# Where the side work of a mixture-of-experts stage is put between its pairs: fixed shares of a chunk instead of one interleaved list

## The chip, the cores and the metric

The kernel runs on one core of a Trainium2 chip. The time is the device time of one execution, in microseconds (us). The core has five engines with a queue of instructions each: TensorE (PE) multiplies matrices, VectorE (DVE) and ScalarE (ACT) work on elements, GpSimd (POOL) does some element work and issues some DMAs, and SyncE (SP) issues most DMAs. Each engine takes its own instructions in the order in which the program gives them, and waits for the others through semaphores.

## The reference

The input is an image batch of 2 x 256 channels x 64 x 64, read as two sequences of 4096 tokens. Three things are added to it in turn:

```
x = x + L0(gn(x))                  # a selective scan (Mamba), 256 channels
t = tokens(x)
t = t + attn(ln(t))                # a forward and a backward selective scan, 512 channels
t = t + ffn(ln(t))                 # the mixture of experts, the last stage below

def ffn(x):                        # x: 2 batches, 4096 tokens, 256 channels
    feat = mean(x, axis=0)         # over the two batches
    w = softmax(feat @ Wr + br)    # one weight per token and expert, 8 experts
    h = relu(bn(einsum('bfd,edh->bfeh', x, W1) + b1))
    h = relu(bn(einsum('bfeh,ehk->bfek', h, W2) + b2))
    y = einsum('bfeh,ehd->bfed', h, Wo) + bo
    return einsum('bfed,fe->bfd', y, w)
```

Every expert is computed for every token, and the router's weight w of a token is shared by the two batches, since it comes from their mean.

## The kernel before

Channels lie on partitions, 128 at a time (KC = 2 halves), and tokens are cut into 8 chunks of 512. The first and far longer part of the kernel runs the scans of all six jobs slot by slot. Into free slots it already places expert work for chunks whose tokens are finished, and stores each expert's unweighted result u in DRAM. In this kernel that covers all eight experts of batch 0 in every chunk, and of batch 1 in chunks 7 and 6.

The last stage, which the change touches, therefore has two kinds of chunk. `whole` holds chunks 7 and 6, of which everything is stored. `rest` holds chunks 5, 4, 3, 2, 1, 0, of which batch 1 is still to be computed. The stage walks over `pairs` (b, i, e), batch, chunk and expert: eight pairs, all of batch 1, for each chunk of `rest`, 48 in all. One turn of this loop does the following, in this order on every engine:

- `layer` twice (L1203): two halves with two matmuls each into a PSUM tile hp (L1208), and ACT's relu into h (L1212).
- `weigh` (L1218) of the pair before: DVE multiplies its h by the router's weights wb of its expert (L1219).
- `last_layer` (L1221) of the pair three turns back: eight matmul rows into y (L1227). After a chunk's eighth pair DVE adds y to x (L1232) and SP stores x to the output (L1182).
- Some items of the chunk's side work, a list of functions `side[i]`.

The side work consists of these items. `routes(j)` prepares the router of a chunk that comes later, in five steps:

- `load_n` (L1083): POOL issues the load of the normalized tokens n of both batches (L1093). A chunk that is already loaded is passed over.
- `layer_norm` (L1095): does nothing for a chunk whose normalized tokens were stored earlier, which is all but batch 1 of chunk 0.
- `both` (L1113): POOL adds the two batches into nm (L1115). There is one buffer of nm.
- `logits` (L1117): PE multiplies nm by Wr into lt (L1122); DVE, ACT (the exp, L1137) and DVE make the softmax w (L1127 to L1141).
- `spread` (L1143): PE transposes w (L1147), ACT copies it to wts (L1149), POOL writes that to DRAM (L1151) and loads it back to all partitions as wb (L1153, 2 MB). There are two buffers of wb.

`sums(j)` adds the stored results of a chunk to its tokens: `load_x` (SP loads x of both batches, L1163), `bias` (PE multiplies wts by bo, L1170; ACT copies, L1171; POOL adds it to x, L1173), then `add_early` for each stored expert (SP loads u, L1177; DVE multiplies it by wb, L1178, and adds it to x, L1179), and `store` (L1182) for a batch of which all experts were stored. A chunk of `rest` has 11 such items with eight adds, a chunk of `whole` 20 with sixteen. u has three buffers, x and n six each.

Before the change the list of chunk number `at` of `rest` is built at once (L1241 to L1254): first the sums of the whole chunk whose router was made during the chunk before, then the sums of the chunk itself mixed with the steps of `routes` of the next whole chunk and of the next chunk of `rest`, one step after every `every` sums. The loop takes an equal part of what is left after each pair (L1290); for the first chunk it begins after the third pair. So chunk 5 has the routes of 7 and 4, chunk 4 the sums of 7 and 4 and the routes of 6 and 3, chunk 3 the sums of 6 and 3 and the routes of 2; chunks 2 and 1 have their own sums and the routes of 1 and 0, and chunk 0 its own sums.

Of the kernel before, what the change touches and what calls it, by code (L numbers as in the profile page):

```python
# [131 lines left out]
def hybrid_kernel(ctx: ExitStack, tc: tile.TileContext, a: dict, out: bass.AP):  # L132
# [53 lines left out]
    with ExitStack() as st:  # L186
# [826 lines left out]
        done = []  # L1013
        for g in range(nq):
            i, jp, n = quads[g]
# [49 lines left out]
    with ExitStack() as st:  # L1065
# [11 lines left out]
        rest, whole = [], []  # L1077
# [5 lines left out]
        def load_n(i):  # L1083

            if (0, i) in n:
                return
            for b in range(NB):
                n[b, i] = mk.tile([P, KC, T], F32, tag="n", name=f"n_{i}{b}", bufs=6)
                if (b, i) in featured:
                    src = nf_dram[b][:, i, :, :]  # L1090
                else:
                    src = t_dram[b][:, :, i * T : (i + 1) * T]
                nc.gpsimd.dma_start(n[b, i], src)  # L1093

        def layer_norm(i):  # L1095
            for b in range(NB):
                if (b, i) in featured:
                    continue
                v = n[b, i]
                mean = psp.tile([P, T], F32, tag="ps", name=f"mean_m{i}{b}")  # L1100
                for k in range(KC):
                    nc.tensor.matmul(mean, mean_w, v[:, k, :], start=(k == 0), stop=(k == KC - 1))
                nc.vector.tensor_tensor(v, v, over_channels(mean), ALU.subtract)
                sq = mk.tile([P, KC, T], F32, tag="u", name=f"sq_{i}{b}", bufs=3)
                nc.scalar.activation(sq, v, AF.Square)
                var = psp.tile([P, T], F32, tag="ps", name=f"var_m{i}{b}")
                for k in range(KC):
                    nc.tensor.matmul(var, mean_w, sq[:, k, :], start=(k == 0), stop=(k == KC - 1))
                r = mk.tile([P, T], F32, tag="r", name=f"r_{i}{b}", bufs=1)
                rsqrt(r, var, eps5)  # L1110
                nc.vector.tensor_tensor(v, v, over_channels(r), ALU.mult)

        def both(i):  # L1113
            n["sum", i] = mk.tile([P, KC, T], F32, tag="nm", name=f"nm_{i}", bufs=1)
            nc.gpsimd.tensor_tensor(n["sum", i], n[0, i], n[1, i], ALU.add)  # L1115

        def logits(i):  # L1117

            lt = psp.tile([P, q, E], F32, tag="ps", name=f"lt_{i}")
            for t in range(q):  # L1120
                for k in range(KC):
                    nc.tensor.matmul(  # L1122
                        lt[:, t, :], n["sum", i][:, k, t * P : (t + 1) * P], wr[:, k, :],
                        start=(k == 0), stop=(k == KC - 1),
                    )
            w = n["w", i] = mk.tile([P, q, E], F32, tag="w", name=f"w_{i}")
            nc.vector.tensor_tensor(  # L1127
                w, lt, br.rearrange("p (o e) -> p o e", o=1).to_broadcast([P, q, E]), ALU.add
            )
            mx = mk.tile([P, q], F32, tag="mx", name=f"mx_{i}")  # L1130
            nc.vector.tensor_reduce(mx, w, AX.X, ALU.max)

            def over_experts(v):
                return v.rearrange("p (q o) -> p q o", o=1).to_broadcast([P, q, E])

            nc.vector.tensor_tensor(w, w, over_experts(mx), ALU.subtract)
            nc.scalar.activation(w, w, AF.Exp)  # L1137
            sm = mk.tile([P, q], F32, tag="sm", name=f"sm_{i}")
            nc.vector.tensor_reduce(sm, w, AX.X, ALU.add)
            nc.vector.reciprocal(sm, sm)  # L1140
            nc.vector.tensor_tensor(w, w, over_experts(sm), ALU.mult)  # L1141

        def spread(i):  # L1143

            pt = psp.tile([P, T], F32, tag="ps", name=f"wt_{i}")
            for t in range(q):
                nc.tensor.transpose(pt[:E, t * P : (t + 1) * P], n["w", i][:, t, :], ident)  # L1147
            wts[i] = mk.tile([E, T], F32, tag="wt", name=f"wts_{i}", bufs=3)
            nc.scalar.copy(wts[i], pt[:E, :])  # L1149
            w_dram = drp.tile([E, T], F32, name=f"w_dram{i}")  # L1150
            nc.gpsimd.dma_start(w_dram, wts[i])  # L1151
            wb[i] = mk.tile([P, E, T], F32, tag="wb", name=f"wb_{i}")
            nc.gpsimd.dma_start(  # L1153
                wb[i], w_dram.rearrange("e (o t) -> o e t", o=1).to_broadcast([P, E, T])
            )

        def routes(i):
            return [lambda: load_n(i), lambda: layer_norm(i), lambda: both(i), lambda: logits(i), lambda: spread(i)]

        def load_x(i):  # L1160
            for b in range(NB):
                x[b, i] = mk.tile([P, KC, T], F32, tag="x", name=f"x_{i}{b}", bufs=6)
                nc.sync.dma_start(x[b, i], t_dram[b][:, :, i * T : (i + 1) * T])  # L1163

        def bias(i):

            bi = mk.tile([P, KC, T], F32, tag="bi", name=f"bi_{i}", bufs=1)
            for m in range(KC):
                ps = psp.tile([P, T], F32, tag="ps", name=f"bi_{i}_{m}")
                nc.tensor.matmul(ps, bo[:, m * P : (m + 1) * P], wts[i], start=True, stop=True)  # L1170
                nc.scalar.copy(bi[:, m, :], ps)  # L1171
            for b in range(NB):
                nc.gpsimd.tensor_tensor(x[b, i], x[b, i], bi, ALU.add)  # L1173

        def add_early(b, i, e):
            u = mk.tile([P, KC, T], F32, tag="u", name=f"u_{b}{i}_{e}", bufs=3)
            nc.sync.dma_start(u, u_dram[b, i, e])  # L1177
            nc.vector.tensor_tensor(u, u, over_channels(wb[i][:, e, :]), ALU.mult)  # L1178
            nc.vector.tensor_tensor(x[b, i], x[b, i], u, ALU.add)  # L1179

        def store(b, i):
            nc.sync.dma_start(  # L1182
                out[b].rearrange("(k p) l -> p k l", p=P)[:, :, i * T : (i + 1) * T], x[b, i]
            )

        def sums(i):

            work = [lambda: load_x(i), lambda: bias(i)]
            for b in range(NB):
                work += [lambda b=b, e=e: add_early(b, i, e) for e in range(first[b, i])]  # L1190
                if first[b, i] == E:
                    work.append(lambda b=b: store(b, i))
            return work
# [5 lines left out]
        def load_w(name, e):  # L1199
            we[name, e] = mw.tile([P, KC, C], F32, name=f"{name}_{e}")  # L1200
            nc.sync.dma_start(we[name, e], a[name][e].rearrange("(k p) n -> p k n", p=P))
# [16 lines left out]
        def weigh(b, i, e, h):  # L1218
            nc.vector.tensor_tensor(h, h, over_channels(wb[i][:, e, :]), ALU.mult)  # L1219
# [18 lines left out]
            (b, i, e) for i in rest  # L1238
            for e in (order if i == rest[0] else range(E)) for b in range(NB) if e >= first[b, i]
        ]  # L1240
        side = {i: [] for i in rest}  # L1241
        for at, i in enumerate(rest):
            after = rest[at + 1 : at + 2]
            now, work = sums(i), side[i]
            if at:
                for j in whole[at - 1 : at]:
                    work += sums(j)
            ahead = []
            for j in whole[at : at + 1] + after:
                ahead += routes(j)  # L1250
            every = max(1, len(now) // max(1, len(ahead)))
            while now or ahead:
                work += ahead[:1] + now[:every]
                ahead, now = ahead[1:], now[every:]  # L1254

        load_n(rest[0])
        for name, e in [("W1", order[0]), ("W2", order[0]), ("W1", order[1]), ("W2", order[1])]:
# [12 lines left out]
        done = {i: 0 for i in rest}  # L1270
        count = {i: sum(p[1] == i for p in pairs) for i in rest}
        for at, (b, i, e) in enumerate(pairs):
            for name, k in weights[: 6 if at else 4]:
                load_w(name, k)
            weights = weights[6 if at else 4 :]
            h = layer(n[b, i], 0, e, f"{i}_{e}_{b}")
            h = layer(h, 1, e, f"{i}_{e}_{b}")
            if at == 0:
                logits(i)
            elif at == 1:  # L1280
                spread(i)

            for p in {0: [], 1: [], 2: waiting[:1], 3: waiting[1:]}.get(at, waiting[-1:]):
                weigh(*p)
            waiting.append((b, i, e, h))
            if len(waiting) > 3:
                last_layer(*waiting.pop(0))
            done[i] += 1
            work = side[i] if at > 1 else []
            upto = -(-len(work) // (count[i] - done[i] + 1))  # L1290
            for fn in work[:upto]:
                fn()
            side[i] = side[i][upto:]
        weigh(*waiting[-1])
        for p in waiting:
            last_layer(*p)
# [104 lines left out]
```

## Time and profile before

| what | value |
|---|---|
| median of 3 runs | 5132.12 us (5131.54 to 5132.48) |
| the profiled execution | 5134.52 us |
| its span, first to last instruction | 5132.7 us |
| mean granted TensorE clock | 0.917 of full speed |
| busy: PE, DVE, ACT, POOL | 4283.0, 4581.7, 3681.3, 4410.3 us |
| last stage, 4537 to 5133 us: PE busy | 559.85 of 596 us |
| of these, chunk 5, 4537 to 4629 us: PE, DVE, ACT, POOL busy | 85.25, 34.44, 27.75, 16.88 us |
| chunk 4, 4629 to 4742 us | 97.25, 70.39, 28.74, 19.17 us |
| chunk 3, 4742 to 4844 us | 96.83, 73.71, 27.79, 14.72 us |
| chunks 2, 1 and 0, 4844 to 5133 us | 280.53, 101.74, 85.12, 24.90 us |

The profile is of one execution. A row of it names a line of the kernel, an engine, an operation and its tiles (output, arrow, inputs), with a time on that engine; an entry in square brackets tells how long the engine sat idle before the row and which instruction of which engine ended that wait. "SPq" is the time in which SP issues a DMA, not the time of its transfer. The times of the whole chunks in the table are windows of the timeline, cut at the first hp of a chunk.

### The profile page before, as it was taken

The numbers are of one execution on the slowest core, as the hardware profiler recorded it, in microseconds if no ns is written. First come the engines' busy times: TensorE is split into PE (matmuls) and PEld (weight loads), VectorE is DVE, ScalarE is ACT, GpSimd is POOL, SyncE is SP. The second block draws the span as 40 slices with busy tenths as digits, with TensorE's granted clock in tenths as the row PEclk, the third lists the DMA queues.
The fourth block names the chain that finished last, engine by engine and source line by source line (L and its number), as shares of the span: only waits on it lengthen the run. The fifth ranks groups of instructions, "written<-read, shape, count | busy, mean of one in ns | idle before, by whom it ended". The sixth has DMA issues, their size and how long they took to land.

```text
span 5132.7 us, 47350 instructions
## 1 busy us (share of the span) xinstructions
PE 4283.0 (83%) x14920; PEld 1485.7 (29%) x14920; DVE 4581.7 (89%) x3088; ACT 3681.3 (72%) x7474; POOL 4410.3 (86%) x1442
## 2 busy tenths in 40 slices
PE   5677767776668988888988888899999999888999
PEld 1222222221122323333322233233333333333444
DVE  6998999999999999999989999999999999936543
ACT  5777677777767888888888788888778878832232
POOL 5998999999999999999989999999999999911100
PEclk8888888887888999999999999999999999999999
DMA  5454433344444454546654555455554444455532
GB/s 178 149 176 158 164 136 128 132 146 144 151 139 156 170 195 163 184 165 209 207 185 170 174 181 179 159 167 177 195 187 166 167 165 161 168 180 182 191 108 77
DMA packets 321355, 845.49 MB, mean 165 GB/s; under 512 B 35720, under 2 KB 107152, under 8 KB 279120
## 3 DMA queue, kind: packets, MB, share of 16 engines
q1 hardware_dynamic: 316816, 815.07, 46.2%
q0 software_dynamic: 4288, 27.40, 1.4%
q8 instruction: 118, 1.93, 0.2%
q14 instruction: 133, 1.09, 0.1%
HBM read 655.05 MB, written 187.30 MB: 164 GB/s over the span
## 4 chain that ended last, share of the span: by engine, by line
DVE 20%; PE 15%; ACT 10%; issue 4%; POOL 3%; DMA 2%; SPq 0%; DVEq 0%; POOLq 0%; ACTq 0%
DVE da L690 9%; PE hp L1208 5%; DVE bq L699 5%; ACT da L664 4%; PE y L1227 2%; PE e L912 2%; DVE bq L690 2%; POOL bq L654 2%; PE conv L452 1%; POOL bq L715 1%; PE y L723 1%; ACT bq L675 1%; DVE x L1179 1%; DVE u L1178 1%; ACT eh L923 1%
## 5 line engine op out<-in xcount | busy, mean ns | idle before, releaser
L654 POOL TENSOR_TENSOR bq<-rxdt,bc 128x2048 f32<-128x2048 f32 x640 | 2893.2, 4543 | 28.7 <-issue 12.3
L664 ACT ACTIVATE da<-rdt,w_a 128x512 f32<-128x512 f32 x2560 | 1756.8, 686 | 105.4 <-DVE bq L690 59.8
L690 DVE TENSOR_TENSOR_SCAN da<-da,h_state,bq 128x1024 f32<-128x1024 f32 x664 | 1559.1, 2348 | 50.5 <-ACT da L664 34.4
L715 POOL TENSOR_TENSOR bq<-bq,bc 128x2048 f32<-128x2048 f32 (+1 forms) x280 | 1179.9, 4214 | 22.5
L690 DVE TENSOR_TENSOR_SCAN bq<-da,h_state,bq 128x1024 f32<-128x1024 f32 x456 | 1059.3, 2338 | 28.5 <-ACT da L664 28.4
L723 PE MATMUL y<-bq,stack 128*32 128x512 f32 x5120 | 759.4, 687 | 317.4 <-POOL bq L715 297.3
L699 DVE TENSOR_TENSOR bq<-da,bc 128x1024 f32<-128x1024 f32 x760 | 926.5, 1219 | 16.0
L912 PE MATMUL e<-eh,ew 128*128 128x512 f32 x1280 | 626.1, 620 | 66.0 <-DVE sp L513 15.0
L709 ACT COPY h_state<-da 128x2 f32<-128x2 f32 x759 | 119.1, 157 | 641.3 <-DVE bq L699 639.4
L675 ACT ACTIVATE bq<-h_state,bq,a 128x1 f32<-128x1 f32 x1120 | 430.5, 384 | 0.6
L723 PEld LDWEIGHTS y<-bq,stack 128*32 128x32 f32 x5120 | 143.6, 119 | 876.7 <-POOL bq L715 404.9
L1212 ACT ACTIVATE h<-hp,of,sc 128x512 f32<-128x512 f32 x192 | 149.1, 777 | 298.9 <-PE hp L1208 281.7
L912 PEld LDWEIGHTS e<-eh,ew 128*128 128x128 f32 x1280 | 230.3, 193 | 452.0 <-issue 219.4
L414 PE MATMUL xs<-nx,w_in 128*128 128x512 f32 x640 | 318.7, 628 | 40.9 <-DVE xc L466 20.8
L452 PE MATMUL conv<-xs,w_conv 64*64 64x512 f32 x2560 | 332.6, 613 | 21.9 <-ACT xs L436 18.9
L414 PE MATMUL z<-nx,w_in 128*128 128x512 f32 x640 | 323.8, 639 | 18.7 <-DVE sp L513 10.6
L912 PE MATMUL e<-en,ew 128*128 128x512 f32 x640 | 308.3, 613 | 23.9 <-DVE fcen L809 7.8
L761 PE MATMUL o<-sz,w_out 128*128 128x512 f32 x640 | 301.7, 612 | 0.0
L923 ACT ACTIVATE eh<-e,of,sc 128x512 f32<-128x512 f32 x320 | 242.1, 768 | 36.7 <-PE e L912 36.2
L517 POOL TENSOR_TENSOR xdt<-sp,xc 128x512 f32<-128x512 f32 x160 | 203.2, 1273 | 49.9 <-DVE sp L513 49.8
L730 PE MATMUL y<-xc,w_d 128*128 128x512 f32 x320 | 193.1, 688 | 54.2 <-DVE sz L742 53.9
L690 DVE TENSOR_TENSOR_SCAN da<-da,bq 128x1024 f32<-128x1024 f32 x96 | 219.4, 2286 | 6.5 <-ACT da L664 3.6
(139 smaller groups left out, 4940.5 us busy)
## 6 DMA issues: line engine op xcount, KB each, us to landing
rxdt<-xdtd SPq DMA_DIRECT2D x160, 1024.0 KB, 6.8
rdt<-dtd SPq DMA_DIRECT2D x160, 1024.0 KB, 6.5
bc<-bcd SPq DMA_DIRECT2D x384, 256.0 KB, 3.2
dtd<-sp SPq DMA_DIRECT2D x160, 256.0 KB, 3.5
xdtd<-xdt SPq DMA_DIRECT2D x160, 256.0 KB, 4.0
ew<-in_W SPq DMA_DIRECT2D x160, 256.0 KB, 4.3
u<-u SPq DMA_DIRECT2D x80, 512.0 KB, 4.4
u<-eu SPq DMA_DIRECT2D x76, 512.0 KB, 4.0
```

Source lines behind the costliest of these rows:

```text
L414: nc.tensor.matmul(ps, job.w["in", half][:, k, j * P : (j + 1) * P], rhs, start=(k == 0), stop=(k == KC - 1),)
L452: nc.tensor.matmul(v[r][64 * col : 64 * col + 64, :], job.w["conv"][rows, 2 * jp + j, k, :], ck["xs", jp][rows, j, k : k + T] if k < 4 els ...
L654: nc.gpsimd.tensor_tensor(bq[g], ck["rxdt", j], over_groups(ck["bc", 0, sg]), ALU.mult)
L664: nc.scalar.activation(da[g, h][:, k, :], cks[i]["rdt", j][:, q, :], AF.Exp, scale=steps[i][0].w["a"][:, j, q * SG + sg : q * SG + sg + 1],)
L675: nc.scalar.activation(bq[g][:, q, 0:1], job.h[:, j, sg, q : q + 1], AF.Identity, scale=cks[i]["a0", j][:, h, sg : sg + 1], bias=bq[g][:, ...
L690: nc.vector.tensor_tensor_scan(b if on_pool(g, h) else d, d, b, job.h[:, j, sg, 2 * h : 2 * h + 1] if c else 0.0, ALU.mult, ALU.add,)
L699: nc.vector.tensor_tensor(bq[g][:, two, :], d, cks[i]["bc", 1, sg].rearrange("p (o t) -> p o t", o=1).to_broadcast([P, 2, T]), ALU.mult,)
L715: nc.gpsimd.tensor_tensor(b, b, cks[i]["bc", 1, sg].rearrange("p (o t) -> p o t", o=1).to_broadcast([P, groups, T]), ALU.mult,)
L723: nc.tensor.matmul(y[i, j][q * CG : (q + 1) * CG, :], stack, bq[g][:, q, :], start=False, stop=(sg == SG - 1),)
L761: nc.tensor.matmul(v[m], job.w["out"][:, j, m * P : (m + 1) * P], ck["sz", j], start=False, stop=(j == job.nj - 1),)
L912: nc.tensor.matmul(ps, ew[l][:, k, m * P : (m + 1) * P], key[x][:, k, :], start=(k == 0), stop=(k == KC - 1),)
L923: nc.scalar.activation(key[dst][:, m, :], key["ps", l, m], AF.Relu, bias=of[:, l, e, m : m + 1], scale=sc[:, l, e, m : m + 1],)
```

## The change

The list of a chunk is now made of items with a share between 0 and 1, sorted by it. The five steps of `routes` get the shares 0, 0.2, 0.3, 0.55 and 0.8; where a whole chunk and a chunk of `rest` are both prepared, the second one's are 0.1 later. The sums, those of the whole chunk first as before, are spread evenly from 0.1 on. After each pair the loop runs every item whose share is below the part of the chunk's pairs that is done, and after the last pair all that is left. As before, the first chunk begins after its third pair. Nothing else is changed, and the same instructions are issued.

```diff
-        side = {i: [] for i in rest}
+        side = {}
         for at, i in enumerate(rest):
-            after = rest[at + 1 : at + 2]
-            now, work = sums(i), side[i]
+            side[i] = []
+            for k, j in enumerate(whole[at : at + 1] + rest[at + 1 : at + 2]):
+                for part, fn in zip((0, 0.2, 0.3, 0.55, 0.8), routes(j)):
+                    side[i].append((part + 0.1 * k, fn))
+            now = sums(i)
             if at:
-                for j in whole[at - 1 : at]:
-                    work += sums(j)
-            ahead = []
-            for j in whole[at : at + 1] + after:
-                ahead += routes(j)
-            every = max(1, len(now) // max(1, len(ahead)))
-            while now or ahead:
-                work += ahead[:1] + now[:every]
-                ahead, now = ahead[1:], now[every:]
+                now = [fn for j in whole[at - 1 : at] for fn in sums(j)] + now
+            side[i] += [(0.1 + 0.9 * k / len(now), fn) for k, fn in enumerate(now)]
+            side[i].sort(key=lambda work: work[0])
...
             done[i] += 1
-            work = side[i] if at > 1 else []
-            upto = -(-len(work) // (count[i] - done[i] + 1))
-            for fn in work[:upto]:
-                fn()
-            side[i] = side[i][upto:]
+            while at > 1 and side[i] and (done[i] == count[i] or side[i][0][0] < done[i] / count[i]):
+                side[i].pop(0)[1]()
```

## The prediction

> **What bounds the kernel now.** The page first: TensorE and VectorE share the load until the last stage, where the second half of the PE row is full and the DVE row falls off. I then asked for the chain of waits, restricted to the last stage (from 4537 us), for the waits of PE there, and for the timeline around each wait. In the chain, PE (L1208, L1227) carries the stage almost alone: a pair of batch and expert costs 10.57 us on PE (4652.20 to 4662.77), 48 pairs. What PE loses is in these waits (engine, line, what it waited for: us in total, times, longest):
>
> ```profile
> PE lt L1122 <- POOL nm L1115: 16.3, 2, 12.4
> PE hp L1208 <- DMA W<-in_W: 13.7, 1, 13.7
> PE wt L1147 <- DVE w L1141: 3.3, 2, 1.7
> PE var_m L1108 <- ACT sq L1105: 2.4, 1, 2.4
> PE hp L1208 <- ACT h L1212: 1.2, 1, 1.2
> ```
>
> The weight wait opens the stage and var_m belongs to the layer norm of the last chunk; neither is touched. The others lie in the second and third chunk (numbers 4 and 3). Timeline around the first (start, duration, what; in brackets idle before and its releaser):
>
> ```profile
> 4695.99 1.39 SPq L1163 DMA_DIRECT2D x<-t_dram  x2
> ...
> 4701.19 4.63 POOL L1173 TENSOR_TENSOR x<-x,bi 128x1024 f32<-128x1024 f32 x2 [53.21 <-DMA x<-t_dram]
> 4703.63 3.27 DVE L1178 TENSOR_TENSOR u<-u,wb 128x1024 f32<-128x1024 f32 x1 [6.97 <-DMA u<-u]
> 4705.79 3.31 POOL L1115 TENSOR_TENSOR nm<-n,n 128x1024 f32<-128x1024 f32 x1
> ...
> 4709.15 3.58 PE L1122 MATMUL lt<-wr,nm 128*128 128x8 f32 x16 [12.37 <-POOL nm L1115]
> ...
> 4712.77 0.19 DVE L1127 TENSOR_TENSOR w<-lt,br 128x32 f32<-128x32 f32 x1 [1.45 <-PE lt L1122]
> ```
>
> PE needs nm; nm stands on POOL behind the bias add of chunk 4, which waited for x; x was asked for late because SP stood behind sums that DVE had not done. Note that DVE itself reached the softmax of this lt only at 4711.3, where its last multiply before it (L1219, from 4710.10) ends. The second place shows what then happens:
>
> ```profile
> 4829.41 6.25 PE L1208 MATMUL hp<-n,W 128*128 128x512 f32 x8
> ...
> 4835.24 0.18 DVE L1127 TENSOR_TENSOR w<-lt,br 128x32 f32<-128x32 f32 x1
> ...
> 4835.90 0.23 ACT L1137 ACTIVATE w<-w 128x32 f32<-128x32 f32 x1 [16.45 <-DVE w L1136]
> 4836.04 1.43 ACT L1212 ACTIVATE h<-hp,of,sc 128x512 f32<-128x512 f32 x2
> ...
> 4836.85 3.70 PE L1208 MATMUL hp<-h,W 128*128 128x512 f32 x8 [1.20 <-ACT h L1212]
> ```
>
> The exp of the softmax stands on ACT ahead of the next relu, so **a late DVE stops PE**: PE resumes 1.6 us after DVE begins w.
>
> What these places cost: chunks 4 and 3 run from 4628.93 to 4844.26, 215.3 us. Their work is 16 pairs at 10.57, four bi at 2.1 (1.91 and small gaps), three lt at 1.75, three wt at 0.44: 184.1. The excess is **31.2 us**: 20.8 of idle (12.4, 1.65, 1.65, 3.9, 1.2) and 10 of slow matmuls after it.
>
> **What the Trainium skill says.** "TensorE: Matmul & The Clock Gate", What's actually happening: an idle window of about 3.4 us halves the clock until PE has been busy for about as long. The trace agrees: after 13.73 us of idle eight hp took 5.59 us instead of 3.43. The same page, Architectural detail: ACT and DVE are strict FIFO; the exp above agrees. "GPSIMD Engine Reference", 1. Specifications: POOL's SBUF interfaces are shared with VectorE for instructions with two SBUF inputs; here the multiply took 3.27 us beside POOL, 1.22 alone. "DMA: Bandwidth & Descriptors", Anatomy of one DMA: a semaphore wait is done by the issuing sequencer before dispatch; here each store that waits for DVE holds back the loads behind it on SP.
>
> **The change part by part.** No instruction is added or removed; the built order of the two kernels differs only in the last stage.
>
> *Logits and the sum of n ahead of the bias add.* In chunk 4 POOL now has bias(7), both(6), both(3), bias(4); in chunk 3 bias(6), both(2), bias(3). nm is ready some 10 us after the first bias add (4.65 + 3.3) while lt stands two to three pairs later, and n is loaded at the chunk's start. both(3) has to wait for lt(6), the one nm buffer, but lt(3) comes a pair (10.6) later and nothing else stands behind it on POOL. So lt<-nm falls away. spread is two pairs behind logits in all chunks, so wt<-w (3.3) falls away too. All 31.2 us of the old places are gone.
>
> *Where is DVE when the new lt comes?* This decides. Sums of the whole chunk (16) no longer stand first; in chunk 4 the first four adds come in pair 1, with their bias. I set 0 at the chunk's first hp. PE: two pairs 21.1, bi, three pairs, lt(6) at the end of pair 4: ends at 56.7. Ahead of that softmax DVE has 13 adds, three weigh and one final add. From these rows:
>
> ```profile
> 4639.61 1.98 PE L1170 MATMUL bi<-wts,bo 8*128 8x512 f32 x4
> ...
> 4644.66 3.36 DVE L1179 TENSOR_TENSOR x<-x,u 128x1024 f32<-128x1024 f32 x1 [9.69 <-POOL x L1173]
> ...
> 4668.52 1.22 DVE L1232 TENSOR_TENSOR x<-y,x 128x1024 f32<-128x1024 f32 x1
> 4675.08 1.23 DVE L1178 TENSOR_TENSOR u<-u,wb 128x1024 f32<-128x1024 f32 x1 [5.34 <-DMA u<-u]
> ```
>
> bi to first x add: 5.05, so 21.1 + 5.05 = 26.2 (before: PE issued that bi one pair sooner, at 10.7). First add to 29.6 (3.36 beside POOL); nm now follows at once on POOL and takes 2.3 in between; adds two to four at 2.39 (4675.08 to 4677.55 and on): 39.0; weigh and the final add, 1.15 each: 41.3. On SP the store of chunk 5 now stands between load four and five, so the loads start after the final add: 5.4 empty as in the row above, 46.7. Four adds: 56.3. The store of the first half: 5.4 again (a weigh inside it), 61.7. Three adds, weigh, two adds: 74.8. Here w(6) begins, **18 us after lt(6) ended**. PE can do one layer of the next pair meanwhile (3.43) and resumes at 74.8 + 1.6 = 76.4 instead of 60.1: 16.3 us idle, then the slow clock, 2.15 by the row of the stage's start: 18.4 us.
>
> Chunk 3 has the same list with chunk 6, the same place of lt(2) and again nm behind the bias on POOL: 18.4. It begins with the weights wb waiting for the last weigh of chunk 4; that weigh ends about 5 into chunk 3, POOL issues the load 2 later (1.8 in the waits) and it lands in 9.5 (median of wb's issues), at about 17; its x load by about 21, ahead of 23.8 when POOL needs x. lt(3), in the pair after the stall, finds DVE in time (its last add ends at about 82, lt(3) at 85).
>
> Chunk 5: first adds come in pair 2 after the first weigh (wb at 4576), two adds and two weigh end by 4587, y needs them at 4589; lt at the ends of pairs 4 and 5 find DVE idle. Nothing. Chunks 2, 1, 0: eight adds each; DVE reaches lt's softmax at about 53 against 56. Nothing. The last adds and the store end pairs before the closing 13.75 us of y. Nothing; without that cover, an add is 2.4.
>
> Sum: -31.2 + 2 x 18.4 = **+5.6 us**. The profiled execution has a span of 5132.7 (5134.5 with what lies around it; median of the runs 5132.1, 2.4 below). So span 5138.3 and median 5137.7; I say **5138**.
>
> **Unknown costs.** The wait of a load behind one store: 5.34 after the final add, up to 7.03 where two stores were just ahead; I take 5.4, its nearest case. POOL's nm between two adds: 0 to 2.3; I take 2.3. Slow clock: 1.7 (after 1.65 idle) to 2.8 (the row of 6.25); I take 2.15. All low: (14.0 + 1.7) x 2 = 31.4, +0.2. All high: (19.5 + 2.8) x 2 = 44.6, +13.4.
>
> **Rivals.** A measurement of this kernel tells about 0.2%, 10.3 us, from no change.
> 1. *The stall changes its releaser but keeps its size* (forecast): chance 0.54, 5126 to 5142.
> 2. *Slower*: the two empty stretches behind stores on SP are 7.0 each. Place: the loads L1177 after each L1182 in chunks 4 and 3; price: 3.2 more per chunk and the dearer clock, 5145.5; it decides from 6.6 per stretch on (each stall 2.3 longer), or when x of chunk 6 lands after 23.8 in the crowd of wb, n and u loads at that chunk's start (a load of u took 13.9 in such a crowd at 4748). For it: 6.97 and 7.03 were seen; against: those stood behind two transfers. Chance 0.38.
> 3. *Faster*: DVE reaches w(6) by 58.5, nothing stops PE, -31.2: 5101. For: DVE is busy for only 70 of 113 us in chunk 4, and 13 adds stand ahead of it where 17 stood. Against: it needs 16 us that I find nowhere: the bias comes a pair later, lt a pair sooner. Chance 0.08.
> That the change doesn't do what it says is excluded by the built order.
>
> **Numbers.** Faster 0.08, same 0.54, slower 0.38, from the three cases. The range 5126 to 5156 holds the forecast's own 5126 to 5142 and most of the slower case with its crowd of loads; outside are the faster case and 0.08 above.
>
> **What would show it.** Right: PE lt<-POOL nm and wt<-DVE w gone from the waits; instead two waits hp L1208<-ACT h of about 16 us, one in chunk 4 near 4689 to 4705, one in chunk 3; ACT w<-DVE w long in the same places; DVE u<-DMA u about 5.4 behind stores. Wrong, if these hp waits are below 8 us or absent (rival 3), or above 19 (rival 2), or if lt still waits for POOL.

## The result and the profile after

| | before | after |
|---|---|---|
| median of 20 runs | 5131.53 us (5127.63 to 5136.37) | 5138.72 us (5133.62 to 5146.66) |
| after to before, 95% interval | | 1.0014 (1.0008 to 1.0021) |
| span of the profiled execution | 5132.7 us | 5131.9 us |
| first hp of the last stage | 4543.67 us | 4537.72 us |
| from there to the end | 589.0 us | 594.2 us |
| chunk 5 / 4 / 3 | 85.3 / 113.0 / 102.3 us | 86.2 / 111.1 / 110.2 us |
| chunks 2, 1 and 0 with the closing y | 288.4 us | 286.7 us |

The changed kernel is slower by 0.14%, 4 to 11 us: less than the 0.2% that the prediction set as the bound of a difference, but with an interval clear of 1. The two spans alone would say the opposite. The profiled execution of the changed kernel, 5133.62 us, was the fastest of its 20, and it reached the last stage 6 us sooner than the other profile did, in code that the change does not touch. So the last stage is measured from its first hp: it took **5.2 us longer**.

The waits of PE in the last stage, after (engine, line, what it waited for: us in total, times, longest):

```profile
PE hp L1208 <- ACT h L1212: 32.9, 2, 16.9
PE hp L1208 <- DMA n<-nf_dram: 12.1, 1, 12.1
PE var_m L1108 <- ACT sq L1105: 2.4, 1, 2.4
```

The waits for nm (16.3) and for w (3.3) are gone. The 1.2 us of hp<-ACT h have become 32.9 in two waits, one in chunk 4 and one in chunk 3. The timeline of chunk 4 (start, duration, what; in brackets idle before and its releaser), which begins at 4623.91, shows where the first one comes from:

```profile
4645.16 1.98 PE L1170 MATMUL bi<-wts,bo 8*128 8x512 f32 x4
...
4650.22 3.35 DVE L1179 TENSOR_TENSOR x<-x,u 128x1024 f32<-128x1024 f32 x1 [9.26 <-POOL x L1173]
...
4652.46 3.33 POOL L1115 TENSOR_TENSOR nm<-n,n 128x1024 f32<-128x1024 f32 x1
...
4653.50 3.37 DVE L1178 TENSOR_TENSOR u<-u,wb 128x1024 f32<-128x1024 f32 x1
...
4663.96 1.22 DVE L1232 TENSOR_TENSOR x<-y,x 128x1024 f32<-128x1024 f32 x1
...
4665.21 0.39 SPq L1182 DMA_DIRECT2D out<-x  x1
...
4665.65 7.65 SPq L1177 DMA_DIRECT2D u<-u  x4
...
4670.47 1.22 DVE L1178 TENSOR_TENSOR u<-u,wb 128x1024 f32<-128x1024 f32 x1 [5.29 <-DMA u<-u]
...
4678.91 1.85 PE L1122 MATMUL lt<-wr,nm 128*128 128x8 f32 x16
...
4680.16 0.39 SPq L1182 DMA_DIRECT2D out<-x  x1
...
4680.61 3.68 PE L1208 MATMUL hp<-n,W 128*128 128x512 f32 x8
...
4685.41 1.23 DVE L1178 TENSOR_TENSOR u<-u,wb 128x1024 f32<-128x1024 f32 x1 [4.14 <-DMA u<-u]
...
4698.59 0.18 DVE L1127 TENSOR_TENSOR w<-lt,br 128x32 f32<-128x32 f32 x1
...
4699.26 0.23 ACT L1137 ACTIVATE w<-w 128x32 f32<-128x32 f32 x1 [22.80 <-DVE w L1136]
4699.39 1.43 ACT L1212 ACTIVATE h<-hp,of,sc 128x512 f32<-128x512 f32 x2
...
4700.21 5.67 PE L1208 MATMUL hp<-h,W 128*128 128x512 f32 x8 [15.91 <-ACT h L1212]
```

PE has lt done at about 4680.6, for nm was there long before (POOL's row of 4652.46). DVE comes to the softmax of that lt only at 4698.59, 18.0 us later, because its adds stand ahead of it and the adds stop at every store: SP issues the store of a sum and only then the loads behind it, so that after each of the two stores the next multiply sits waiting (5.29 and 4.14 us). ACT stands idle at the exp for 22.80 us, the two relus behind it run one after the other from 4699.39, and PE has stood for 15.91 us. In chunk 3 the end of the same chain:

```profile
4812.29 5.95 PE L1208 MATMUL hp<-h,W 128*128 128x512 f32 x8 [16.94 <-ACT h L1212]
```

### The profile page after: what moved, and what is told of

The parts are those of the page before. It is cut to its first block, busy times and chain, and to the rows that moved or that the text cites. A ratio compares the mean times of both kernels' runs of the same rounds, so it can differ in the third digit from the quotient of the medians.

```text
span 5131.9 us, 47348 instructions
## 1 busy us (share of the span) xinstructions
PE 4267.0 (83%) x14920; PEld 1477.3 (29%) x14920; DVE 4584.4 (89%) x3088; ACT 3681.6 (72%) x7474; POOL 4412.3 (86%) x1442
## 4 chain that ended last, share of the span: by engine, by line
DVE 26%; PE 18%; ACT 13%; issue 5%; POOL 4%; DMA 3%; SPq 0%; DVEq 0%; POOLq 0%; ACTq 0%
DVE da L690 12%; DVE bq L699 6%; ACT da L664 6%; PE hp L1208 5%; PE e L912 3%; DVE bq L690 3%; POOL bq L654 3%; PE y L1227 2%; PE conv L452 2%; PE y L723 2%; ACT bq L675 1%; PE o L761 1%; POOL bq L715 1%; DMA dtd<-sp 1%; DMA u<-u 1%
```

## The experiments

Seven kernels in two groups; each group was timed beside the kernel before, whose median was 5132.61 us in the first (softmax split, bias first, stores behind, all three) and 5131.46 us in the second (the other three). The stage is measured in each profile from its first hp to the end.

| kernel | median, us | to before, 95% | stage, us | chunk 4, 3, us | PE idle in chunk 4; 3, us |
|---|---|---|---|---|---|
| before | (see above) | | 589.0 | 113.0, 102.3 | 15.7; 5.1 |
| after | 5138.72 | 1.0014 (1.0008 to 1.0021) | 594.2 | 111.1, 110.2 | 15.9; 16.9 |
| nm first (before, one edit) | 5129.81 | 0.9998 (0.9990 to 1.0006) | 586.9 | 109.8, 103.8 | 14.8; 8.7 |
| softmax split | 5118.41 | 0.9973 (0.9961 to 0.9984) | 576.1 | 93.3, 109.8 | 0; 14.9 |
| bias first | 5132.41 | 0.9999 (0.9991 to 1.0007) | 590.4 | 111.9, 105.3 | 12.3; 12.8 |
| stores behind | 5120.25 | 0.9978 (0.9968 to 0.9988) | 575.9 | 103.6, 99.9 | 8.3; 6.3 |
| stores and bias | 5107.93 | 0.9952 (0.9939 to 0.9964) | 564.5 | 98.8, 91.8 | 2.3; 0.7 |
| stores and split | 5100.71 | 0.9937 (0.9924 to 0.9951) | 558.7 | 93.3, 91.1 | 0; 0 |
| all three | 5101.38 | 0.9940 (0.9926 to 0.9953) | 558.1 | 93.3, 91.1 | 0; 0 |

My theory: DVE sets the pace of chunks 4 and 3. The exp on ACT, ahead of the relus, is what passes its lateness on to PE, and the wait that ends last (nm before, the relu after) is only the place where it shows. Rival A: the place itself is the loss, so that taking away that wait brings the time back. Rival B: DVE simply has too much work in these two chunks, so that no order helps.

### Before, with nm alone put first

Does the wait for nm cost anything of its own? The kernel before, with one edit, which takes POOL's sum `both` out of its place in the lists of chunks 4 and 3 and puts it ahead of the chunk's own bias:

```diff
             while now or ahead:
                 work += ahead[:1] + now[:every]
                 ahead, now = ahead[1:], now[every:]
+            if at in (1, 2):
+                work.insert({1: 23, 2: 22}[at], work.pop({1: 24, 2: 26}[at]))
```

> The kernel before with one edit: in chunks 4 and 3 POOL's sum of n (nm) is put ahead of the chunk's own bias add, nothing else moved. Theory (DVE sets the pace, nm was only the wait that ended last): lt<-POOL nm of 12.4 and 3.9 us go, but PE then waits at wt<-DVE w in chunk 4 (lt and wt stand in one pair there) for some 10 us and at hp<-ACT h in chunk 3 for some 6, because DVE reached those softmaxes only at 4711.3 and 4835.2; what is gained is nm no longer running beside a multiply, 2 us per chunk: 5128. Rival (the late nm was itself the loss): the 31 us go, 5101.

The waits of PE in its last stage:

```profile
PE wt L1147 <- DVE w L1141: 14.8, 2, 13.2
PE hp L1208 <- DMA n<-nf_dram: 12.1, 1, 12.1
PE hp L1208 <- ACT h L1212: 8.7, 1, 8.7
PE var_m L1108 <- ACT sq L1105: 2.4, 1, 2.4
```

and the timeline of chunk 4 around lt:

```profile
4696.42 1.85 PE L1122 MATMUL lt<-wr,nm 128*128 128x8 f32 x16
...
4709.86 0.18 DVE L1127 TENSOR_TENSOR w<-lt,br 128x32 f32<-128x32 f32 x1
...
4711.46 1.02 PE L1147 MATMUL wt<-ident,w 128*8 128x128 f32 x4 [13.19 <-DVE w L1141]
```

lt<-POOL nm has left the list: lt runs at 4696.42 instead of 4709.15. DVE begins the softmax at 4709.86 (4712.77 before), and PE stands 13.19 us at the transpose in place of 12.37 at lt. In all 23.5 us of idle in place of 20.8; the stage is 2.1 us shorter, and the medians can't be told apart. Rival A falls for the old wait: of the 31 us around it, the wait for nm held some 2. The two waits came out larger than I expected (13.2 and 8.7 for some 10 and 6). The expectation had them too small for its own times of DVE: PE is done with lt at 4698.3, and a softmax begun at 4711.3, with PE 1.6 later, would have meant 14.6 in chunk 4.

### The softmax split

```diff
         def logits(i):
...
             nc.vector.tensor_tensor(w, w, over_experts(mx), ALU.subtract)
+        def softmax(i):
+            w = n["w", i]
             nc.scalar.activation(w, w, AF.Exp)
...
-                for part, fn in zip((0, 0.2, 0.3, 0.55, 0.8), routes(j)):
+                for part, fn in zip((0, 0.2, 0.3, 0.4, 0.55, 0.8), routes(j)):
```

Lt and DVE's part up to the subtraction now stand at share 0.4, the exp and what follows at 0.55. (In the kernels without the split, lt and the whole softmax stand at 0.55.) So the exp keeps its place among the relus on ACT; it is lt and the steps of DVE ahead of it that come a pair sooner. Both the distance between them and the number of adds ahead of DVE's steps change.

> The changed kernel with the softmax cut in two: lt and the DVE steps up to the subtraction at share 0.4, the exp and the rest at 0.55, so that the exp stands on ACT about a pair behind the DVE steps it waits for. DVE gets no less work and no fewer waits. Theory (a late DVE stops PE through the exp that stands ahead of the relus on ACT): the two waits of hp for ACT h (15.9 and 16.9 us in the changed kernel) and the slow clock after them go, at most 4 us of waits remain in chunks 4 and 3; 5139 - 33 = about 5106 us, about 0.5% faster than before. Rival (what limits these chunks is the rate of DVE and its loads, the exp is only where it shows): PE waits as long elsewhere, at y for the weighted h; 5135 to 5142.

A part of it came, 5118 for the expected 5106. In chunk 4 PE has no wait. DVE begins the softmax there 59.3 us after the chunk's first hp, with eight adds ahead of it (74.7 and thirteen in the changed kernel), and the exp is done in time:

```profile
4684.31 0.18 DVE L1127 TENSOR_TENSOR w<-lt,br 128x32 f32<-128x32 f32 x1
...
4684.98 0.23 ACT L1139 ACTIVATE w<-w 128x32 f32<-128x32 f32 x1 [5.66 <-DVE w L1132]
```

Chunk 3 keeps a wait of 12.05 us (some lines have moved; hp is L1210, the weighing L1221, the exp L1139):

```profile
4744.78 1.22 DVE L1221 TENSOR_TENSOR h<-h,wb 128x1024 f32<-128x1024 f32 x1
...
4757.75 1.22 DVE L1221 TENSOR_TENSOR h<-h,wb 128x1024 f32<-128x1024 f32 x1 [11.75 <-DMA wb<-w_dram]
...
4792.70 0.18 DVE L1127 TENSOR_TENSOR w<-lt,br 128x32 f32<-128x32 f32 x1
```

and on PE:

```profile
4765.73 1.95 PE L1122 MATMUL lt<-wr,nm 128*128 128x8 f32 x16 [1.03 <-POOL nm L1115]
4775.13 3.70 PE L1229 MATMUL y<-h,Wo 128*128 128x512 f32 x8 [0.20 <-DVE h L1221]
4794.31 6.74 PE L1210 MATMUL hp<-h,W 128*128 128x512 f32 x8 [12.05 <-ACT h L1214]
```

PE now goes through chunk 4 in 93.3 us in place of 111.1 and is at chunk 3 at 4718.27. DVE has not become faster over the whole of chunk 4: its last weigh of chunk 4 begins 26.5 us after the first hp of chunk 3 (8.0 in the changed kernel). The load of wb waits for that weigh (the buffer), the next weigh for wb (11.75), and the softmax of chunk 3 comes 25 us after lt is done. PE can go on for some 15 us after lt now, a pair and a layer (one layer in the changed kernel), and that is spent. So the exp is how DVE stops PE, and the split moves the stop on to the next chunk as long as DVE keeps its rate. Which of its two parts did more in chunk 4, the distance or DVE's earlier steps, was not tested: the whole softmax at 0.4 in one piece was not run.

### The bias first

The whole chunk's x load and bias (from shares 0.1 and 0.13) to the first pair; the load, at 0.1, stood there already, so it is the bias that moves:

```diff
-            side[i] += [(0.1 + 0.9 * k / len(now), fn) for k, fn in enumerate(now)]
+            side[i] += [
+                (0.01 * k if k < 2 and at and whole[at - 1 : at] else 0.1 + 0.9 * k / len(now), fn)
+                for k, fn in enumerate(now)
+            ]
```

> The changed kernel with load_x and bias of the whole chunk at share 0, so in pair 0 as in the kernel before, and not in pair 1; all else stays. Theory: DVE may begin its adds at 17 instead of 26.2 us into the chunk, loses 3 of that again at the final add, which waits for y of pair 2 (33.8), and reaches the softmax at 68.5 instead of 74.8: each of the two waits shrinks by about 6, to 10; 5139 - 13 = about 5126 us. Rival (the start of the adds isn't what sets the softmax; the loads are): waits unchanged within 1 us, 5139.

The waits of PE, its two rows, and behind them DVE's first weigh in chunk 4 (the chunk begins at 4627.90):

```profile
4700.55 6.77 PE L1208 MATMUL hp<-h,W 128*128 128x512 f32 x8 [12.27 <-ACT h L1212]
4812.94 5.20 PE L1208 MATMUL hp<-h,W 128*128 128x512 f32 x8 [12.79 <-ACT h L1212]
...
4642.41 2.27 DVE L1219 TENSOR_TENSOR h<-h,wb 128x1024 f32<-128x1024 f32 x1 [16.14 <-DMA wb<-w_dram]
```

12.27 for 15.91 and 12.79 for 16.94: some 4 us of DVE's time each, not 6. The first add of chunk 4 came at 20.2 us into it, not at 17: DVE's order has this weigh ahead of it, which had wb only at 14.5, and it and the multiply behind it (2.27 and 3.37 us for 1.22) fell on POOL's bias add. Chunk 3 is 4.9 us shorter than in the changed kernel, but chunk 4 is 0.8 us longer although its wait is 3.6 shorter: the clock was slow there for longer (last section). The median is 5132 for the expected 5126.

### The stores behind

A store whose sum was just made is what SP waits at. Every store of a batch of stored sums is issued three adds later, and that of the final add, in `last_layer`, at the end of its turn of the loop (the last lines of the diff, which also stand after the loop). The function `behind` moves the stores of sums in the list:

```diff
+            now = behind(now)
...
-                store(b, i)
+                late.append((b, i))
...
+            while late:
+                store(*late.pop())
```

> The changed kernel with every store of L1182 issued on SP a few loads of u later than in the changed kernel (three adds later, or after the turn's other items for the store after the final add), so that no load of u stands behind a store that waits for DVE. Theory: the two empty stretches of 5.4 us on DVE ahead of the softmax go, DVE reaches it at 64 instead of 74.8 us, the waits of hp shrink from 16 to about 5.5 each; 5139 - 22 = about 5117 us. Rival (the loads are limited by their rate, not by their place): DVE waits for u as long in other places, 5135 to 5139.

DVE's wait for u in the last stage, ahead of it that of the changed kernel:

```profile
DVE u L1178 <- DMA u<-u: 57.1, 12, 7.3
```

```profile
DVE u L1178 <- DMA u<-u: 8.9, 3, 4.2
```

and PE's two waits:

```profile
4693.77 5.81 PE L1219 MATMUL hp<-h,W 128*128 128x512 f32 x8 [8.34 <-ACT h L1223]
4795.38 6.21 PE L1219 MATMUL hp<-h,W 128*128 128x512 f32 x8 [6.32 <-ACT h L1223]
```

No DVE instruction was removed, and the waits halved: 15.9 to 8.3 and 16.9 to 6.3. Rival B falls here: another order helps, and a large part of DVE's lateness was want of loads and not work (it begins the softmax of chunk 4 at 67.1 us, 7.6 sooner). The waits were expected at some 5.5. Whether more than three buffers of u, or stores issued on another queue than the loads, would do the same was not tried.

### Two of the three together, and all

> The changed kernel with the stores three sums later and the whole chunk's bias first, the softmax in one piece. Theory (the lateness of DVE is a sum: first add late, two empty stretches, each counts): waits of 8.3 and 6.3 (stores alone) fall by the 3.6 that the early bias brought, to about 4.5 and 2.5, slow clock less: 5112. Rival: gains don't add, DVE is held by weights wb and by its own work: 5119.

> The changed kernel with the softmax split off (exp three tenths of a chunk... here at share 0.4) and the stores three sums later, but the biases where they were. Theory: both repairs together are enough and the early bias was not needed: the last wait of 12 us in chunk 3 (splitting alone left it) goes, since DVE gains 10 us per chunk from the stores: 5103, no hp<-ACT h above 2 us. Rival: DVE is still late in chunk 3, since PE gets further ahead of it: 5108 to 5110 with a wait of 5 or more there.

> The three edits together. Theory: DVE reaches the softmax before PE's relus need the exp, no wait of hp for ACT over 2 us remains in chunks 4 and 3; 5139 - 37 = about 5102 us, the fastest of the four by a few us at most over the split alone. Rival (rate of DVE): PE waits at y or at the final adds of these chunks, 5115 or more.

With stores and bias, the waits are 2.34 and 0.73 us. The two together gain more than the sum of the edits alone (3.6 + 7.6 of 15.9 in chunk 4, 4.1 + 10.6 of 16.9 in chunk 3 would leave 4.7 and 2.2); why the early bias brings more when the loads flow was not followed further. With stores and split, the list of PE's waits is down to the stage's start and the layer norm:

```profile
PE hp L1221 <- DMA n<-nf_dram: 13.5, 1, 13.5
PE var_m L1108 <- ACT sq L1105: 2.4, 1, 2.4
```

and with all three it is the same, with 13.9 at the start. The split needs the stores (alone it leaves 12.05 us in chunk 3); the early bias adds nothing to the two. **Stores and split beat both kernels**: 5100.71 us, 0.9937 of before (0.9924 to 0.9951). The two chunks then take 184.4 us, where the prediction had put their work at 184.1: all of the old excess of 31.2 us is gone, and the medians are 30.8 us (stores and split) and 31.2 us (all three) below the kernel before.

## Why the prediction was right

Predicted 5138, measured 5138.72; predicted +5.6 for the last stage, measured +5.2 in the profiles and 7.2 between the medians. That the absolute figure is met within 1 us is in part luck: over 20 runs the kernel before came out 0.6 lower than over the three the prediction started from, and the difference 1.6 higher. By its steps:

- **The old waits.** lt<-POOL nm and wt<-DVE w are gone, as predicted. The experiment with nm first adds what the prediction said in one sentence ("DVE itself reached the softmax of this lt only at 4711.3"): before the change, too, DVE came to the softmax too late, and without the wait for nm PE stands for DVE instead (23.5 us of idle in all, 20.8 with it).
- **The time of DVE.** Counted from the chunk's first hp: lt done at 56.7 (predicted 56.7), first add at 26.3 (26.2), loads there again after the first store at 46.6 (46.7), after the second at 61.5 (61.7), w at 74.7 (74.8). The multiply beside nm took 3.37, the 2.15 more that were put at 2.3. The two empty stretches behind stores were 5.29 and, with the weigh of 1.14 between, 5.3: the nearest row before was the right one to take, and the 7.0 of the slower rival did not come. That the stretches come from the place of the stores is shown by the kernel with the stores behind.
- **The price of the stall.** 16.3 of idle and 2.15 of slow clock each, against 15.9 and 16.9 of idle. The slow clock is what is left of the two chunks' 221.3 us over 184.4 of work and 32.9 of idle: 4.0, 2.0 each. "TensorE: Matmul & The Clock Gate", What's actually happening, in the Trainium skill, agrees on the hp after the stall, 5.67 and 5.95 us in place of 3.43 to 3.7. That this term came out so near is partly luck: for the waits of 6 us and more in the other runs it was 1.4 to 6.3 a chunk (below).
- **Chunk 3.** "The same list" held to 1 us: w at 75.7. What was off is the step "that weigh ends about 5 into chunk 3": it ended at 9.2, so wb and the weigh that needs it came at 20.6 in place of 17, and the first add at 27.5. The adds and the wait for the stores follow as in chunk 4. And the "load of u" of 13.9 us in the crowd at 4748 was DVE's wait for it in the kernel before; the crowd that the slower rival feared did not hold up x: POOL's bias add began at 23.9, and what it had waited for was bi.
- **Chunks 5, 2, 1 and 0, "nothing".** No wait of PE was added or taken there. They differ by +0.9 and -1.7 us all the same. Practically all of it is the clock after waits that both kernels have: the first eight hp took 6.68 for 5.75 us, and the four matmuls of var_m 1.98 for 3.68 after the same 2.40 us of idle. So of the +5.2, +6.0 is the change's (215.3 to 221.3; predicted +5.6) and -0.8 is from elsewhere.
- **The rivals.** The faster one asked for 16 us of DVE "that I find nowhere". They were to be found: 7.6 and 10.6 in the stores' places, 4 in the bias, or, with the split, 15.4 by putting DVE's part of the softmax ahead of five adds (59.3, where the rival asked for 58.5). In the changed kernel itself none of these is done. The size that rival gave, 31.2 us below before, is what the combined kernel reached.

## What to carry to other kernels

When a wait at one engine ends last, look at when the other inputs of that same work would have been there: here removing the wait for nm gained 2 us of 31, since DVE came to the softmax 11.6 us after lt in any case. A short step on an in-order engine that waits for a late one (the exp ahead of the relus, a store ahead of loads) spreads the lateness to everything behind it, so issue it only when what it needs is likely done; two such moves together gave 31 us against the kernel before, either alone 12 to 14. And compare the changed stage from a common start within the traces: total spans carried 6 us of difference from before the change's first instruction.

## What the runs showed of the hardware that I had not expected

The same short wait brings the slow clock in one run and not in another. After 2.40 us of idle ahead of var_m, four matmuls (before, after, and stores and bias with the hp that follows):

```profile
4960.76 3.68 PE L1108 MATMUL var_m<-sq,mean_w 128*128 128x512 f32 x4 [2.40 <-ACT sq L1105]
```

```profile
4961.71 1.98 PE L1108 MATMUL var_m<-sq,mean_w 128*128 128x512 f32 x4 [2.40 <-ACT sq L1105]
```

```profile
4934.65 2.60 PE L1108 MATMUL var_m<-sq,mean_w 128*128 128x512 f32 x4 [2.40 <-ACT sq L1105]
4937.04 4.72 PE L1219 MATMUL hp<-n,W 128*128 128x512 f32 x8
```

The 2.60 is no smaller price: the hp behind it took 4.72 us in place of 3.60. From the start of var_m to the y that follows, 1.7 us were lost (1.64 to 1.70) in six of the nine profiles, and nothing in the other three (after, softmax split, stores behind). The Trainium skill, "TensorE: Matmul & The Clock Gate", What's actually happening, says that the window is free-running and that the slow stretch therefore differs from run to run. The rows agree as to where it falls and whether it comes; what it costs here is 1.7 us or nothing. They also show that 2.4 us of idle, shorter than the window of about 3.4 us, can be enough.

In the kernel with the bias first the clock fell a second time, 12 us after the stall and with PE busy throughout:

```profile
4700.55 6.77 PE L1208 MATMUL hp<-h,W 128*128 128x512 f32 x8 [12.27 <-ACT h L1212]
4707.15 3.60 PE L1227 MATMUL y<-h,Wo 128*128 128x512 f32 x8
4710.59 1.85 PE L1122 MATMUL lt<-wr,nm 128*128 128x8 f32 x16
4712.36 2.61 PE L1170 MATMUL bi<-wts,bo 8*128 8x512 f32 x4
4714.91 6.41 PE L1208 MATMUL hp<-n,W 128*128 128x512 f32 x8
```

y ran at full speed, then bi and the next eight hp took 2.61 and 6.41 where 1.98 and 3.70 are usual. The stall's slow clock came to 6.3 us in that chunk (111.9 less 93.3 of work less 12.3 of idle), against 1.4 in chunk 3 of the same run. What starts the second fall was not found. The rows ahead of it are lt and bi, narrow matmuls of 8 columns and of 8 rows; the changed kernel has the same five rows after its stall in chunk 4, and there bi and hp took 1.98 and 3.70, so they alone don't bring it. The fall can eat a gain of the size of the bias edit.

A second finding is on DVE. Beside POOL's nm, which ran from 4589.71 to 4592.06 in the changed kernel, a subtraction of 128x32 elements, 0.19 us elsewhere, took as long as what was left of POOL's instruction:

```profile
4589.71 2.35 POOL L1115 TENSOR_TENSOR nm<-n,n 128x1024 f32<-128x1024 f32 x1 [14.53 <-issue]
...
4590.06 2.05 DVE L1136 TENSOR_TENSOR w<-w,mx 128x32 f32<-128x32 f32 x1
```

It ended at 4592.11, as POOL's did. The multiply of 4653.50 fits the same reading: POOL's nm beside it ended at 4655.79, and the multiply 1.08 later, about its own 1.22. So in these rows an instruction of DVE that falls on one of POOL's is not slowed in proportion to its own size; it loses what is left of the other.
